# Nearer steps for the third group's tail in layer 0 of a four-layer graph attention kernel

## The chip, the cores and the metric

One core of a Trainium2 chip runs the whole kernel. Its engines are TensorE (PE), VectorE (DVE), ScalarE (ACT) and GpSimd (POOL); SP issues transfers and computes nothing. The metric is the device time of one execution in microseconds (us).

## The reference

There are 3327 nodes with 256 features and a sparse, symmetric adjacency matrix with a full diagonal. Four layers of attention follow one another; each adds its result to its input and norms the sum row by row:

```python
x = _layernorm(x + _L0_gnn_ref(x, adj, ...))   # scores from leaky_relu(g_src[i] + g_tgt[j]) @ a_w
x = _layernorm(x + _L1_gnn_ref(x, adj, ...))   # leaky_relu(s1[i] + s2[j])
x = _layernorm(x + _L2_gnn_ref(x, adj, ...))   # s_src[i] + s_dst[j]
x = _layernorm(x + _L3_gnn_ref(x, adj, ...))   # two layers of four heads each
```

In layer 0 the score of a pair of nodes needs a leaky ReLU over all 256 channels, so it can't be split into a term for each node, and it is formed only for the neighbours that exist:

```python
g = leaky_relu(g_src[:, None, :] + g_tgt[None, :, :], 0.2)
score = where(adj != 0, einsum('ijc,c->ij', g, a_w), -inf)
return softmax(score, axis=1) @ g_tgt
```

## The kernel before, in words

The nodes make 26 tiles of 128 rows. Layer 0 (`sparse0`, L288) treats them in four groups of 4, 7, 9 and 6 tiles (`SETS`); the third group is tiles 11 to 19. For each group `neighbours` lists every node's neighbours, and the nodes of a group are sorted by their number of neighbours, so that tile t of a group needs only as many places as `LEVELS` says. A tile's places are cut into parts of up to four (`parts`, L318, 237 of them). A **step** is one index q of the loop at L1370: it emits what is due at q, then the gathers of part q + 8 (`LEAD`), then the scores of part q.

What a tile passes through:

- `gather` (L916): one indirect GpSimd transfer for each place fetches one neighbour's row for 128 nodes from a table in memory. Its buffers are 22 in a ring.
- `score` (L956): VectorE takes the maximum with the own row (L946) and multiplies and sums (L952), place by place.
- `weights` (L980): VectorE finds the maximum (L985), ScalarE the exponential (L990), after the tile's last part.
- `combine` (L1013): ScalarE scales the gathered rows by their weights (L1028), PE adds them up in PSUM by a multiplication with the identity (L1031). For the very last tile, VectorE adds the parts from the fifth on instead (`add_aside`, L1007 and L1009).
- `add_input` (L1046): VectorE divides and adds the input. Its result lies in one of two buffers (tag "hs"), which `dots_next` (L1142) also uses for the weights of layer 1.
- `put_back` (L1062): an indirect GpSimd transfer writes the sums to memory in the nodes' own order. It is put into a list, `between`, from which one is taken after every second gather (L932), so it stands among the gathers of GpSimd's queue.

What a group passes through once its last tile is put back: `take` (L1073) loads the sums again from ScalarE's queue; `finish_sums` (L1081) forms mean and variance on VectorE; `finish_root` (L1103) takes the root on GpSimd; `finish` (L1109) norms on VectorE (L1114).

Then each tile is prepared for layer 1, while layer 0 goes on with later groups: `turn_next` (L1147) transposes it on PE and copies it on ScalarE, `project_next` (L1156) multiplies it by layer 1's weight on PE (L462), forms exponentials and scaled features on ScalarE (L1161 to L1166), stores them from SP's queue (L1168), and at the end of a block of tiles its rates too (L1178). The last group is normed and projected within layer 1 (`last_group`, L1398).

For the tiles of the first two groups (11 of them, `KNOWN`) layer 1's sums over each other are formed early, in the last group's time, in 44 turns from the last group's first step on: `ask_early` (L1188, SP loads), `weigh_early` (L1206, VectorE mask at L1221, ScalarE cast at L1217), `add_early` (L1226, PE at L1234) and, after each three tiles, `keep_early` (L1239), which copies three sums on ScalarE (L1242) and stores them (L1243) through two buffers.

The order is written out by hand: `at_step(q, what)` puts a call into step q, and steps beyond the last part are emitted at the end (L1386). Every engine runs its instructions in the order that they were emitted in. Within layer 0, step q's calls come in the order of their registration: combines, put-backs and finishes before transposes and projections, and these before the early turns.

The distances that the change touches are counted from a tile's last part, q: combine over steps q + 1 to q + 8 (`SPREAD`), `add_input` at q + 10, `put_back` at q + 13; for a group `take` at q + 21, `finish_sums` at q + 27, `finish_root` at q + 33, `finish` at q + 37. For the third group that last q is 181; the last group begins at step 182 and ends at step 236. The third group's transposes start at step 182 + 38 = 220 and go on every second step, each projection two steps after its transpose: 220 to 238.

Layer 1 (`one_head`, L1821) starts with the block of the first four tiles of the third group, with all 26 tiles as sources. Its first loads (a rate row, three adjacency tiles, three feature tiles; L1716, L146, L2187) come in SP's queue behind all of layer 0's loads; its pools lie in memory that layer 0 used. VectorE forms masked weights (L1728), ScalarE casts the adjacency and stores it (L1755, L146), PE adds up (L1845).

Of the kernel before, what the change touches and what calls it, by code (L numbers as in the profile page):

```python
# [32 lines left out]
SETS = (4, 7, 9, 6)  # L33
# [17 lines left out]
def gat_stack(  # L51
# [71 lines left out]
    for lo, hi in ((0, KNOWN), (KNOWN, EARLY), (EARLY, nt)):  # L123
        count = -(-(hi - lo) // 6)
# [163 lines left out]
    def sparse0(lost):  # L288
        GROUP, TURNS, LEAD, SPREAD = 4, 22, 8, 8
        starts = [sum(SETS[:s]) for s in range(len(SETS))]  # L290
        with ExitStack() as s0:
# [19 lines left out]
            def cuts_of(kt):  # L311

                ends = list(range(0, kt, GROUP)) + [kt]
                if kt % GROUP == 1:
                    ends[-2] -= 1
                return list(zip(ends, ends[1:]))
# [449 lines left out]
            between = []  # L766
# [295 lines left out]
            def put_back(s, t):  # L1062

                entry = held.pop((s, t))
                nc.gpsimd.indirect_dma_start(
                    out=sums_d[s][:, :],
                    out_offset=bass.IndirectOffsetOnAxis(
                        ap=entry["lst"][:, KMAX : KMAX + 1], axis=0
                    ),
                    in_=entry["y"][:, :], in_offset=None,  # L1070
                )
# [205 lines left out]
            ends, begins = {}, {}  # L1277
# [9 lines left out]
            def at_step(q, what, *args):  # L1287
                due.setdefault(q, []).append(lambda: what(*args))
# [17 lines left out]
            for q, key in ends.items():  # L1306
                count = len(cuts_of(seats[key]))
                if key[1] == 0:
                    at_step(q + 2, send_weights, key[0])
                    at_step(q + 3, take_weights, key[0])  # L1310
                    at_step(q + 4, combine_excess, key[0])
                for i in range(count):
                    at_step(q + 1 + i * SPREAD // max(count, SPREAD), combine, *key, i)
                at_step(q + 10, add_input, *key)
                at_step(q + 13, between.append, lambda key=key: put_back(*key))
                if key[1] == SETS[key[0]] - 1 and key[0] < len(SETS) - 1:
                    at_step(q + 21, take, key[0])
                    at_step(q + 27, finish_sums, key[0])
                    at_step(q + 33, finish_root, key[0])
                    at_step(q + 37, finish, key[0])  # L1320
            for s, q in begins.items():
                work, at = excess(s), max(q - 2, 0)
                for y in range(12):
                    at_step(at + y, go_on, work)
            at = begins[len(SETS) - 1] - 2 * KNOWN - 3
# [3 lines left out]
            for s in range(len(SETS) - 1):  # L1329
                for it in range(starts[s], starts[s] + SETS[s]):  # L1330
                    at_step(at, turn_next, it)
                    at_step(at + 2, project_next, it)
                    at += 2
                if s == len(SETS) - 3:
                    at = max(at, begins[len(SETS) - 1] + 38)
            at = begins[len(SETS) - 1] + 2
            at_step(at - 2, ask_early, 0)
            at_step(at - 1, ask_early, 1)
# [19 lines left out]
            for s in range(1, len(SETS)):  # L1358
                at = begins[s] - LEAD - 2
# [865 lines left out]
    lost = nodes.tile([P, 2 * nt], F32, name="lost")  # L2225
    nc.vector.memset(lost, 0.0)
    rest = sparse0(lost)
    with ExitStack() as rs:
        layers(rs, EARLY, rest)
# [75 lines left out]
```

## Time and profile before

| what | value |
|---|---|
| median of 3 runs | 3314.23 us (3307.76 to 3329.03) |
| profiled execution | 2906.56 us, span 2904.8 us, mean PE clock 0.887 |
| busy over the span | PE 80%, DVE 73%, ACT 30%, POOL 34% |
| last gather of layer 0 issued | 1322.4 us after the span's start |
| last put-back of layer 0 issued | 1351.7 us |
| rest (layers 1 to 3) | to 2904.8 us |

Times within the execution are us from the span's start. The page gives each engine's busy time, the span in 40 slices of 72.6 us with a digit for the busy tenths, and groups of instructions with count, busy time, mean ns of one, and the idle time before them with what ended most of it. A timeline row is start, length, engine, line, operation, output<-input, form, count, and in brackets the idle time before it and what ended it. The profiled execution is one; the runs of the median were timed without a profile.

### The profile page before, as it was taken

The page shows a single profiled execution, that of the slowest core. Times are in us where ns is not written, and L with a number is a line of the kernel's source. Part 1 is how long each engine was busy: PE and PEld are TensorE (multiplying, and loading weights), DVE is VectorE, ACT ScalarE, POOL GpSimd, SP SyncE. Part 2 cuts the span into 40 slices and gives each one's busy share as a digit, 9 for nine tenths or more (in the row PEclk, how much of TensorE's full clock was granted, in tenths as well). Part 3 has the DMA queues.
Part 4 walks back from the last instruction along what each step waited for, and adds up shares of the span by engine and source line. Part 5 has one row for each costly group of instructions (what it writes and reads, how often), then busy time and mean ns, then how long its engine had stood idle before and what let it go on. Part 6 is the DMA issues. An engine that isn't in the chain of part 4 may idle for free.

```text
span 2904.8 us, 47707 instructions
## 1 busy us (share of the span) xinstructions
PE 2310.4 (80%) x16735; PEld 1545.7 (53%) x16764; DVE 2128.0 (73%) x5634; ACT 866.0 (30%) x2441; POOL 991.7 (34%) x1059
## 2 busy tenths in 40 slices
PE   6466657555552665767899999999999999999997
PEld 4234435433442444645778888863656667534332
DVE  7799799968872856655455421158999999899997
ACT  4145445443432533544344311111011110110111
POOL 2676777777777777772000000000000000000000
PEclk9577778777776887889999999999999999999998
DMA  7795665445544557765767533331222222212211
GB/s 245 204 271 146 184 190 156 140 141 148 161 115 109 126 162 196 199 177 159 219 179 202 169 93 111 105 90 45 78 80 62 75 80 64 71 43 63 60 45 49
DMA packets 207558, 378.52 MB, mean 130 GB/s; under 512 B 38410, under 2 KB 148080, under 8 KB 206288
## 3 DMA queue, kind: packets, MB, share of 16 engines
q1 hardware_dynamic: 119416, 186.29, 22.5%
q0 software_dynamic: 50768, 154.31, 19.3%
q10 hardware_dynamic: 37128, 34.79, 3.6%
q8 instruction: 137, 2.24, 0.3%
q14 instruction: 109, 0.89, 0.1%
HBM read 333.91 MB, written 47.67 MB: 131 GB/s over the span
## 4 chain that ended last, share of the span: by engine, by line
PE 53%; DVE 8%; POOL 6%; DMA 6%; issue 5%; ACT 2%; ACTq 0%; SPq 0%; DVEq 0%; POOLq 0%; another core or an unknown queue 0%
PE acc L1913 18%; PE acc L1845 14%; PE acc L1921 9%; PE acc L1031 7%; POOL g L926 5%; DVE e L1728 3%; DMA g<-table_d,lst 3%; PE misc L1653 3%; DMA at_d<-at 1%; DVE y L952 1%; ACT g L1028 1%; DMA at<-at_d 1%; DVE y L946 1%; PE early L1234 1%; PE misc L1765 0%
## 5 line engine op out<-in xcount | busy, mean ns | idle before, releaser
L926 POOL DMA_INDIRECT g<-table_d,lst x894 | 853.9, 955 | 275.8 <-issue 237.6
L1728 DVE SCALAR_TENSOR_TENSOR e<-rate,feat,at 128x896 f32<-128x896 f32 (+4 forms) x832 | 843.4, 1078 | 59.0 <-PE acc L1921 47.8
L1913 PE MATMUL acc<-e,feat 128*32 128x384 f32 (+2 forms) x6656 | 691.5, 514 | 2.8 <-DVE e L1728 1.4
L1031 PE MATMUL acc<-g,ident 128*128 128x256 f32 x1766 | 484.5, 430 | 70.7 <-ACT g L1028 47.1
L1913 PEld LDWEIGHTS acc<-e,feat 128*32 128x32 f32 x6656 | 307.1, 110 | 294.9 <-issue 157.4
L1031 PEld LDWEIGHTS acc<-g,ident 128*128 128x128 f32 x1766 | 378.9, 219 | 158.2 <-ACT g L1028 64.9
L1921 PE MATMUL acc<-e,feat 128*32 128x384 f32 (+3 forms) x3328 | 383.6, 512 | 0.0
L1028 ACT ACTIVATE g<-g,w 128x256 f32<-128x256 f32 x883 | 367.5, 495 | 15.1 <-ACT at L1217 10.6
L946 DVE TENSOR_TENSOR y<-g,minus_ps 128x1028 f32<-128x1028 f32 (+2 forms) x233 | 273.3, 1173 | 110.0 <-DMA g<-table_d,lst 100.4
L952 DVE SCALAR_TENSOR_TENSOR y<-y,a_ps 128x257 f32<-128x257 f32 x894 | 324.6, 418 | 15.7 <-PE a_ps L810 2.2
L1845 PE MATMUL acc<-feat,e 128*128 128x257 f32 (+1 forms) x1110 | 257.5, 388 | 15.8 <-DVE e L1728 14.6
L1845 PE MATMUL acc<-feat,at 128*128 128x257 bf16 (+2 forms) x2028 | 239.3, 275 | 8.2 <-DMA at<-at_d 7.6
L1845 PEld LDWEIGHTS acc<-feat,e 128*128 128x128 f32 (+1 forms) x1110 | 211.6, 194 | 50.9 <-DVE e L1728 15.3
L1921 PEld LDWEIGHTS acc<-e,feat 128*32 128x32 f32 (+1 forms) x3328 | 162.1, 110 | 131.0 <-issue 88.7
L1845 PEld LDWEIGHTS <-at 128*128 128x128 bf16 (+2 forms) x2028 | 199.6, 100 | 42.4 <-issue 4.7
L563 PE MATMUL v<-code,leads 65*128 65x512 bf16 (+1 forms) x182 | 79.7, 438 | 144.2 <-DVE cand L589 103.3
L589 DVE MAX8 cand<-v 128x8 f32<-128x104 f32 (+2 forms) x858 | 157.1, 258 | 1.1 <-PE v L566 1.1
L1728 DVE SCALAR_TENSOR_TENSOR e<-rate,feat,at_i 128x640 f32<-128x640 f32 (+4 forms) x108 | 95.9, 899 | 82.3 <-DMA at_i<-in_adj_t_dram 27.7
L1706 POOL DMA_DIRECT2D rate3b_d<-rate_rows x4 | 2.1, 520 | 450.2 <-ACT rate_rows L1705 450.2
L1031 PE MATMUL acc<-own_of,ident 128*128 128x256 f32 x52 | 28.6, 650 | 140.3 <-ACT own_of L1028 89.8
L2099 POOL TENSOR_TENSOR rstds<-rstds,minus_half 128x7 f32<-128x7 f32 (+1 forms) x4 | 7.6, 1906 | 381.9 <-DVE rstds L2098 381.9
L261 POOL TENSOR_TENSOR rstds<-rstds,minus_half 128x6 f32<-128x6 f32 (+3 forms) x9 | 12.4, 1381 | 357.8 <-DVE rstds L260 357.8
(259 smaller groups left out, 2055.7 us busy)
## 6 DMA issues: line engine op xcount, KB each, us to landing
adj_i<-in_adj_dram SPq DMA_DIRECT2D x75, 512.0 KB
at<-at_d SPq DMA_DIRECT2D x150, 224.0 KB
at<-at_d SPq DMA_DIRECT2D x75, 192.0 KB
at<-at_d SPq DMA_DIRECT2D x75, 191.8 KB
g<-table_d,lst POOLq DMA_INDIRECT x894, 3.1
at_i<-in_adj_t_dram SPq DMA_DIRECT2D x39, 320.0 KB
at_i<-in_adj_t_dram SPq DMA_DIRECT2D x25, 383.5 KB
at_i<-in_adj_t_dram SPq DMA_DIRECT2D x25, 256.0 KB
```

The lines of the kernel that those rows point to most:

```text
L563: nc.tensor.matmul(v[:, :w], leads[:, b, :], code[:, :w], start=True, stop=False)
L589: nc.vector.max(spread[:, c0 + c, :], view(v[:, :w]))
L926: nc.gpsimd.indirect_dma_start(out=g[:, k - k0, :], out_offset=None, in_=table_d[:, :], in_offset=bass.IndirectOffsetOnAxis(ap=entry["lst" ...
L946: nc.vector.tensor_tensor(y, rows, minus_src[:, None, :].to_broadcast([P, m, dim + 1]), op=ALU.max)
L952: nc.vector.scalar_tensor_tensor(y, y, 1.0, a_ps[:, : dim + 1], op0=ALU.mult, op1=ALU.mult, accum_out=sc)
L1028: nc.scalar.activation(rows, rows, AF.Copy, scale=w[:, k : k + 1])
L1031: nc.tensor.matmul(dst, ident, rows, start=start, stop=stop)
L1653: nc.tensor.matmul(pacc[:pn, : dim + self.extra], ht[:, k, :pn], self.weight[:, k, :], start=(k == 0), stop=(k == kc - 1),)
L1728: nc.vector.scalar_tensor_tensor(e[:pn, : c1 - c0], self.rate[b][:pn, h_of, : c1 - c0], q, at[:pn, : c1 - c0], op0=ALU.max, op1=ALU.mult,)
L1845: nc.tensor.matmul(accs[s][:pn, : dim + 1], a[:pj, s * P : s * P + pn], f[:pj, : dim + 1], start=(j == skip and part == 0), stop=(j == nt ...
L1913: nc.tensor.matmul(accs[x][p][q : q + 32, : hi - lo], f[:pj, at0 : at0 + 32], es[at0 // hd][:pj, lo:hi], start=(j == 0), stop=(j == nt - 1),)
L1921: nc.tensor.matmul(accs[x][pairs][h_of * 32 : (h_of + 1) * 32, : hi - lo], f[:pj, dim + h_of : dim + h_of + 1].to_broadcast([pj, 32]), es[ ...
```

## The change

For the third group alone (`near`), the combines go over six steps instead of eight, `add_input` comes at q + 7 and `put_back` at q + 8, `take`, `finish_sums`, `finish_root` and `finish` at q + 18, 21, 23 and 26. The transposes start at step 182 + 27 = 209 and go on every step, so that they are at 209 to 217 and the projections at 211 to 219. The first two groups and the last keep their distances. No instruction is added or taken away.

```diff
+                near = key[0] == len(SETS) - 2
+                spread = 6 if near else SPREAD
                 for i in range(count):
-                    at_step(q + 1 + i * SPREAD // max(count, SPREAD), combine, *key, i)
-                at_step(q + 10, add_input, *key)
-                at_step(q + 13, between.append, lambda key=key: put_back(*key))
+                    at_step(q + 1 + i * spread // max(count, spread), combine, *key, i)
+                at_step(q + (7 if near else 10), add_input, *key)
+                at_step(q + (8 if near else 13), between.append, lambda key=key: put_back(*key))
                 if key[1] == SETS[key[0]] - 1 and key[0] < len(SETS) - 1:
-                    at_step(q + 21, take, key[0])
-                    at_step(q + 27, finish_sums, key[0])
-                    at_step(q + 33, finish_root, key[0])
-                    at_step(q + 37, finish, key[0])
+                    after = (18, 21, 23, 26) if near else (21, 27, 33, 37)
+                    for y, what in zip(after, (take, finish_sums, finish_root, finish)):
+                        at_step(q + y, what, key[0])
...
                 for it in range(starts[s], starts[s] + SETS[s]):
                     at_step(at, turn_next, it)
                     at_step(at + 2, project_next, it)
-                    at += 2
+                    at += 2 if s < len(SETS) - 2 else 1
                 if s == len(SETS) - 3:
-                    at = max(at, begins[len(SETS) - 1] + 38)
+                    at = max(at, begins[len(SETS) - 1] + 27)
```

## The prediction

> **What bounds the kernel now.** I read the page first, then busy time by stretches, then the timelines of GpSimd, ScalarE, VectorE and the SP queue around the end of layer 0. "Step" is the loop index of the schedule written out at L1370; a step scores one part of up to four neighbours.
>
> ```profile
> POOL 2676777777777777772000000000000000000000
> L926 POOL DMA_INDIRECT g<-table_d,lst x894 | 853.9, 955 | 275.8 <-issue 237.6
> ```
>
> Layer 0 fills the first 18 slices of 72.6 us. GpSimd issues 894 gathers, 0.955 us each and 0.30 us apart. 76% busy is thus its ceiling (1.0 of 1.26 us), and the stretches show it there to the end:
>
> ```profile
> 1180.00:1250.00 70.00, 39.63 (x165) 31.98 (x163) 42.20 (x141) 28.26 (x70) 53.65 (x56) 0.80 0.68 186
> 1250.00:1325.00 75.00, 54.35 (x214) 41.71 (x215) 52.20 (x172) 36.15 (x106) 56.95 (x59) 0.89 0.68 179
> 1325.00:1352.00 27.00, 22.00 (x94) 17.54 (x94) 13.42 (x41) 15.76 (x49) 1.27 (x2) 0.95 0.34 99
> ```
>
> Columns: stretch, length, busy us of PE, weight loads, DVE, ACT, POOL, then PE clock, DMA share, GB/s. POOL is at 77% and 76%, then at nothing, while PE is 81% busy: from 1325 to 1352 a tail runs that GpSimd no longer sets. GpSimd's timeline gives its ends:
>
> ```profile
> 1322.37 0.95 POOL L926 DMA_INDIRECT g<-table_d,lst  x1 [0.30 <-issue]
> 1344.59 1.00 POOL L1065 DMA_INDIRECT sums_d<-hs,lst  x1 [19.96 <-DVE aside L1007]
> 1351.73 0.96 POOL L1065 DMA_INDIRECT sums_d<-hs,lst  x1 [6.14 <-DVE counts L1392]
> ```
>
> The last gather leaves at 1322.4, the last put-back at 1351.7. Layer 1 loads its fourth feature tile at 1354.5, once that landed. The tail in VectorE, ScalarE and SP:
>
> ```profile
> 1327.62 0.96 DVE L946 TENSOR_TENSOR y<-g,minus_ps 128x771 f32<-128x771 f32 x1 [0.97 <-DMA g<-table_d,lst]
> 1329.76 0.18 DVE L985 TENSOR_REDUCE top<-sc 128x1 f32<-128x28 f32 x1
> 1335.68 1.41 DVE L1728 SCALAR_TENSOR_TENSOR e<-rate,feat,at_i 128x512 f32<-128x512 f32 x2 [5.66 <-DMA feats_d<-feat]
> ```
>
> ```profile
> 1322.79 0.37 ACT L1242 COPY part<-early 128x257 f32<-128x257 f32 x1 [3.45 <-DMA part_d<-part]
> 1330.59 0.17 ACT L1161 ACTIVATE feat<-early 128x1 f32<-128x1 f32 x1 [3.72 <-PE early L462]
> 1337.44 0.33 ACT L990 ACTIVATE w<-sc,top 128x28 f32<-128x28 f32 x1
> 1345.17 3.30 ACT L1028 ACTIVATE g<-g,w 128x256 f32<-128x256 f32 x8
> ```
>
> ```profile
> 1328.55 0.32 SPq L1716 DMA_DIRECT2D rate<-rate_d  x1
> ```
>
> The last tile's maximum is there at 1329.94, but its exponential (L990) starts at 1337.44: ScalarE still has to scale rows of the tile before, and between them waits for PE's projections of the third group (L462). Those five projections of steps 230 to 238 are what makes ScalarE and PE late.
>
> **What the Trainium skill says.** "DMA: Bandwidth & Descriptors", section "Anatomy of one DMA": a semaphore wait happens on the issuing sequencer, and most of about 2 us fixed cost is the write's receipt. The trace agrees: GpSimd itself stood 19.96 us before a put-back, and put-backs land in 2.6 to 5.9 us. "Perfetto Trace Analysis", section "Identifying the Most-Contended Engine", takes occupancy for the bottleneck. By that VectorE (70%) would be close to GpSimd (76%); here the 0.30 us between issues makes 76% a full engine, so the trace decides. "TensorE: Matmul & The Clock Gate", section "What's actually happening": PE's clock is throttled unless it is busy. The clock is 0.75 to 0.89 from 1000 to 1325 us and mostly 0.98 to 1.0 after 1500.
>
> **The change, part by part.** It adds no work. It moves instructions of the third group (nine tiles, steps 102 to 181).
>
> (a) Combining over six steps instead of eight, add_input at +7 instead of +10. Same scales (0.41 us a row) and matmuls (0.44 us a row), off GpSimd's path: 0 us. The cover is GpSimd's continuous gathers from 590 to 1323 us. If it were gone, a tile could cost two steps' rows at once, 1.7 us, times nine = 15 us.
>
> (b) put_back at +8 instead of +13. In GpSimd's queue it now stands among the gathers of step e+16, e being the tile's last part, and needs VectorE's step e+7. Everything behind it, all gathers, would wait. By counting gathers against scores in the timelines, GpSimd is 1 to 10 parts ahead; the limit falls from 11 to 9. The 10 is at step 153, where VectorE stands 40.1 us at L1142, because its buffer waits for a put-back. That put-back now comes at about 912 us instead of 939.7, so this standstill shrinks too, and VectorE resumes at about 915 instead of 942. Cost on GpSimd 0; gain 0, for it is hidden under gathers.
>
> (c) take, finish_sums, finish_root, finish at +18, 21, 23, 26 instead of +21, 27, 33, 37. take issues nine loads on ScalarE's queue (5.1 us), three steps earlier: same price, between steps of slack. finish_root is one 1.4 to 1.8 us power on GpSimd, no more than before. But VectorE's finish at step 207 must wait for it, and GpSimd reaches it just before the gathers of part 212, which began at 1196.9. VectorE would be there at 1176, so it stands until about 1198.7: 22 us, against 12.9 us at step 218 before. Then nine norms of 0.39 us, ready at 1202. Behind it wait scores only; GpSimd's gathers go on. 0 us now, a debt of four steps.
>
> (d) Transposes and projections at steps 209 to 219, one tile a step, instead of 220 to 238. Each brings its SP store of features and, twice, of rates, placed ahead of that step's early loads on SP. From the chain around 1271: projection 0.89, four activations 0.72, transposes 0.45, copy 0.37, early cast and store 0.80, four scales 1.7, last row 0.45: 5.4 us a step, against GpSimd's 5.1. So eleven steps end at about 1199.5 + 11 × 5.4 = 1259. With keep_early's wait (5 us) at step 220, step 222's rows end near 1273 (1271.2 before). From there no projection is left: 3.4 us a step instead of 4.4, so step 230's first row comes near 1299 instead of 1304.3.
>
> (e) The tail. keep_early of step 232 starts near 1306 instead of 1318.2, its third copy goes out near 1311, and the rows of steps 233 to 236 (16 × 0.41 = 6.6 us) are scaled before the last gather lands at 1327.6. The last gather itself doesn't move. So the exponential follows the maximum: 1330.7 (with one hoisted op, below) instead of 1337.4, **6.7 us**. From it to the last row it took 12.0 us (1349.4) with a projection in between; now 0.5 + 19 rows × 0.41 + 0.47 = 8.8, **3.2 us**. VectorE's side sum (5.5 us) fits beside it. Sum 9.9 us.
>
> (f) The instruction order of VectorE also changes: the first two layer-1 mask ops (L1728), after the last scores before, now stand inside the scores of parts 235 and 236. They need layer-1 loads that SP issues only when keep_early's last store has landed (5.0 us after its issue), and come 7.1 us after that (1328.55 to 1335.68). With SP free at 1316 they are ready at 1323, ahead of their turn at 1325: cost 0.7 us, counted.
>
> After the tail, layer 1's loads, stores and matmuls keep their order and shift as a whole. Against the profiled execution: 2906.6 − 9.9 = 2896.7. The runs shown have a median 408 us (14%) longer; no view says where those lie. If all stretched alike the gain would be 11.3. I take 10: **3304 us**, 0.3% less.
>
> **The rivals.**
>
> *It stays hidden or is half eaten* (0 to 5 us, about 3311). For it: VectorE starts the nine steps with a 22 us debt, and (d) estimates eleven dependent steps to within 5 us. Against it: 17 steps without projections follow.
>
> *The hoisted mask ops hold the last scores.* If SP gets free at R, the maximum comes at R + 7.1 + 5.1 (two mask ops 1.4, two scores' rest 3.7). Up to R = 1318.5 nothing is lost. At R = 1328.5, where SP got free before, the gain is all gone; beyond it each microsecond is lost time. Ten later gives 3324. For it: a lower clock than the profiled one lengthens (d) most. Against it: five projections less between step 222 and 232.
>
> *More than the tail is won.* If in the runs shown VectorE or PE, not GpSimd, holds parts of layer 0, then (b)'s 27 us (942 to 915) become real: 3314 − 10 − 27 = 3277. Against it: not one gather of the profiled execution from 590 us on waited more than 0.45 us.
>
> *GpSimd stalls at a nearer put-back*: unlikely. The nearest is that of step 159, which GpSimd reaches at about 960; VectorE, resuming at 915 with 2.65 us a step, has its sums by about 936.
>
> **How the numbers follow.** Forecast (6 to 14 us off, 3300 to 3308) 0.55; half eaten 0.2; hoisted ops, slower than before, 0.13 (3315 to 3330); more won 0.12 (3275 to 3298). The range leaves out the far ends of the last two: 3287 to 3324; the likeliest's own is 3300 to 3308. About 1% (33 us) is what a measurement of this kernel can tell from no change. Faster by that 0.07, from the last case's end; slower 0.03, from the mask ops more than 40 us late; same 0.90.
>
> **What would show it.** Right: gathers still end near 1322, no layer-0 projection after 1262, exponential within 1 us of the maximum, last put-back near 1342, same length from there to the end. Wrong: L926 or L1065 waiting for VectorE before 1320; L1728 standing between L946 and L952; the copy at L1242 after 1315; a changed distance from the last put-back to the end.

## The result, and the profile after

The changed kernel takes 3374.44 us (median of 4 runs, 3364.26 to 3376.65) beside 3318.66 us of the kernel before (4 runs, 3307.76 to 3329.03): ratio **1.0153** [1.0111, 1.0196]; brackets behind a ratio hold its 95% interval. The forecast was 3304 in a range of 3287 to 3324. The time went up instead of down, and lies outside the range.

One plain fact is needed to read what follows. The kernel before took about 2907 us in two of the six series of experiments, with a spread of under 20 us over 58 runs, and 3310 to 3331 us (medians) in the others; one chip gave one level in one series and the other in a later one. The profile that the prediction was worked out from (2906.56 us) is of the first kind. The runs that the median was shown for, and the profile of the changed kernel (3376.65 us, span 3374.8), are of the second. I call them the *even* and the *broken* condition. All ratios compare runs within one series.

The page of the changed kernel, GpSimd's line of busy tenths and its gathers:

```profile
POOL 2734645656555555535650000000000000000000
L926 POOL DMA_INDIRECT g<-table_d,lst x894 | 853.7, 955 | 398.3 <-issue 263.2
```

The gathers take what they took (853.7 us against 853.9), but GpSimd stands 398.3 us before them instead of 275.8, and its row of sevens is gone. So the prediction's "not one gather … waited more than 0.45 us" does not hold here. The kernel before, profiled in the broken condition (the run b_before), has 435.7 us there. It, and not the page shown ahead of the prediction, is the kernel to compare with. Busy time by stretches, of b_before and then of the changed kernel: from the gather of part 101, the last one before the third group, to the last gather; to the last put-back; to the end (columns as in the prediction):

```profile
821.00:1714.00 893.00, 429.62 (x1453) 319.63 (x1461) 460.40 (x1713) 272.10 (x734) 531.54 (x556) 0.69 0.44 119
1714.00:1788.00 74.00, 58.68 (x251) 45.98 (x250) 48.58 (x153) 41.19 (x125) 3.36 (x4) 0.95 0.32 90
1788.00:3336.00 1548.00, 1492.12 (x13710) 952.76 (x13709) 1104.72 (x1518) 290.08 (x898) 33.02 (x35) 0.99 0.34 97
```

```profile
814.00:1761.00 947.00, 432.84 (x1530) 320.76 (x1530) 464.02 (x1723) 282.17 (x777) 532.18 (x556) 0.70 0.42 113
1761.00:1825.00 64.00, 45.96 (x183) 37.11 (x182) 47.79 (x153) 32.29 (x81) 3.47 (x4) 0.88 0.30 88
1825.00:3374.00 1549.00, 1494.68 (x13715) 954.72 (x13713) 1105.25 (x1518) 290.41 (x898) 33.46 (x36) 0.99 0.34 97
```

The busy time of GpSimd is equal (531.54 and 532.18 us). The first stretch grows by 54 us, the tail shrinks by 10 us. Layers 1 to 3 stay: from the last put-back to the end it is 1549.8 and 1550.7 us, and 1553.1 us in the even profile. The two spans differ by 38.2 us. The changed kernel reaches part 101 some 7 us earlier, by chance, as it is the same program up to there; the loss is made in the third and the last group of layer 0, and a gain at the tail of about the forecast's size is there beside it. What GpSimd waited for in the first stretch, of b_before and then of the changed kernel (us in total, times, longest):

```profile
POOL sums_d L1065 <- DVE hs L1056: 51.5, 10, 8.7
POOL g L926 <- remote: 46.6, 15, 5.0
POOL sums_d L1065 <- DVE seat L807: 22.8, 2, 11.4
```

```profile
POOL sums_d L1065 <- DVE hs L1056: 146.2, 13, 25.2
POOL g L926 <- remote: 36.1, 12, 5.8
POOL sums_d L1065 <- DVE seat L807: 15.4, 1, 15.4
POOL rstd L1105 <- DVE rstd L1100: 13.7, 1, 13.7
```

GpSimd stands at put-backs (L1065) for VectorE: 161.6 us instead of 74.3, most of it put down to the sums (L1056), up to 25.2 us at one. "PSUM — Partial Sum Buffer", section "Engine vs sequencer instructions", of the Trainium skill says that GpSimd's queue is strictly first in, first out. The trace agrees: below, the gather at 1398.25 starts only behind the put-back at 1396.93, which had stood 19.3 us. One of these waits in the timeline of the changed kernel, engine after engine (rows of ScalarE, PE, VectorE and GpSimd):

```profile
1378.63 0.17 ACT L1161 ACTIVATE feat<-early 128x1 f32<-128x1 f32 x1 [40.13 <-remote]
1382.44 4.89 ACT L1028 ACTIVATE g<-g,w 128x256 f32<-128x256 f32 x12
1383.00 7.25 PE L1031 MATMUL acc<-g,ident 128*128 128x256 f32 x24 [42.26 <-ACT g L1028]
1395.71 0.48 DVE L1052 SCALAR_TENSOR_TENSOR hs<-acc,inv,own_of 128x256 f32<-128x256 f32 x1 [23.95 <-PE acc L1031]
1396.93 1.01 POOL L1065 DMA_INDIRECT sums_d<-hs,lst  x1 [19.32 <-DVE hs L1056]
1398.25 0.96 POOL L926 DMA_INDIRECT g<-table_d,lst  x1 [0.30 <-issue]
```

ScalarE stands 40 us at a projection's exponential, and the profile names nothing that ended the wait ("remote"). Its scales come late, so PE stands 42 us for them, VectorE 24 us for PE's sums, GpSimd 19 us for VectorE, and the next gather comes only then. What a put-back far behind the sums would have kept from GpSimd, the near one hands on. The largest waits without a named releaser, over all engines of the changed kernel from 100 to 1800 us:

```profile
DVE y L952 <- remote: 163.5, 31, 10.1
PE v L563 <- remote: 117.3, 9, 28.0
ACT feat L1161 <- remote: 110.5, 5, 40.1
```

The kernel before in the broken condition has them too (33 kinds of them in that window); the profile ahead of the prediction has a single one, of 0.3 us.

What two of these waits are for can be read all the same. The exponential at 1378.63 reads a bank (`early`) that PE's L462 had written. VectorE's L952 reads what the instruction just before it on VectorE itself, L946, had written. Rows of PE and VectorE of the changed kernel:

```profile
1339.49 1.03 PE L462 MATMUL early<-w,ht 128*128 128x258 f32 x4
1340.36 0.38 PE L1150 MATMUL early<-ident,h 128*128 128x128 f32 x2
1359.70 1.23 DVE L946 TENSOR_TENSOR y<-g,minus_ps 128x1028 f32<-128x1028 f32 x1 [1.31 <-issue]
1368.83 0.42 DVE L952 SCALAR_TENSOR_TENSOR y<-y,a_ps 128x257 f32<-128x257 f32 x1 [7.90 <-remote]
```

The same pair of VectorE in the profile ahead of the prediction:

```profile
999.76 1.22 DVE L946 TENSOR_TENSOR y<-g,minus_ps 128x1028 f32<-128x1028 f32 x1
1001.01 0.42 DVE L952 SCALAR_TENSOR_TENSOR y<-y,a_ps 128x257 f32<-128x257 f32 x1
```

In the broken condition PE's matmuls were over at 1340.74 (a modelled end) and L946 at 1360.93. The trace has the semaphore updates that released the next ones, a semaphore being the counter by which one instruction tells another that it is done, at 1378.61 and 1368.80: 38 and 8 us later. So, as recorded, it is the signal that came late here, even from an engine to itself. Between L946 and L952 VectorE stands 249 us in all in the changed kernel, and 22 us in the profile ahead of the prediction.

### The profile page after: what moved, and what is told of

Read it like the earlier page. It is cut to its first block, busy times and chain, and to the rows that moved or that the text cites. A ratio compares the mean times of both kernels' runs of the same rounds, so it can differ in the third digit from the quotient of the medians.

```text
span 3374.8 us, 47748 instructions
## 1 busy us (share of the span) xinstructions
PE 2376.9 (70%) x16764; PEld 1577.1 (47%) x16764; DVE 2141.2 (63%) x5634; ACT 868.3 (26%) x2441; POOL 992.8 (29%) x1059
## 4 chain that ended last, share of the span: by engine, by line
PE 46%; DVE 16%; another core or an unknown queue 12%; issue 11%; POOL 6%; DMA 5%; ACT 3%; SPq 0%; ACTq 0%; DVEq 0%; POOLq 0%
PE acc L1914 16%; PE acc L1846 12%; PE acc L1922 8%; POOL g L926 5%; PE acc L1031 5%; DVE y L952 4%; DVE y L946 3%; DVE e L1729 2%; PE misc L1654 2%; ACT g L1028 2%; DVE cand L589 2%; DMA g<-table_d,lst 1%; DVE found L597 1%; DVE junk L688 1%
## 5 line engine op out<-in xcount | busy, mean ns | idle before, releaser
L926 POOL DMA_INDIRECT g<-table_d,lst x894 | 853.7, 955 | 398.3 <-issue 263.2
L1031 PE MATMUL acc<-g,ident 128*128 128x256 f32 x1766 | 531.6, 459 | 253.0 <-ACT g L1028 168.3
L1031 PEld LDWEIGHTS acc<-g,ident 128*128 128x128 f32 x1766 | 407.1, 236 | 366.4 <-ACT g L1028 187.1
L952 DVE SCALAR_TENSOR_TENSOR y<-y,a_ps 128x257 f32<-128x257 f32 x894 | 324.7, 419 | 224.5 <-remote 163.5
L946 DVE TENSOR_TENSOR y<-g,minus_ps 128x1028 f32<-128x1028 f32 (+2 forms) x233 | 273.2, 1172 | 28.4 <-issue 23.0
L589 DVE MAX8 cand<-v 128x8 f32<-128x104 f32 (+2 forms) x858 | 168.4, 261 | 86.0 <-issue 78.5
L563 PEld LDWEIGHTS <-leads 65*128 65x128 bf16 x182 | 22.1, 121 | 266.2 <-remote 108.3
L261 POOL TENSOR_TENSOR rstds<-rstds,minus_half 128x6 f32<-128x6 f32 (+3 forms) x9 | 12.4, 1383 | 361.3 <-DVE rstds L260 361.3
```

The lines of the kernel that those rows point to most:

```text
L563: nc.tensor.matmul(v[:, :w], leads[:, b, :], code[:, :w], start=True, stop=False)
L589: nc.vector.max(spread[:, c0 + c, :], view(v[:, :w]))
L926: nc.gpsimd.indirect_dma_start(out=g[:, k - k0, :], out_offset=None, in_=table_d[:, :], in_offset=bass.IndirectOffsetOnAxis(ap=entry["lst" ...
L946: nc.vector.tensor_tensor(y, rows, minus_src[:, None, :].to_broadcast([P, m, dim + 1]), op=ALU.max)
L952: nc.vector.scalar_tensor_tensor(y, y, 1.0, a_ps[:, : dim + 1], op0=ALU.mult, op1=ALU.mult, accum_out=sc)
L1031: nc.tensor.matmul(dst, ident, rows, start=start, stop=stop)
```

## The experiments

"Lead" is by how many parts GpSimd may be ahead of VectorE before a put-back holds it: a put_back emitted at e + x stands among the gathers of part e + x + 8 and needs VectorE's add_input of step e + y, so x + 8 − y: before 11, after 9. The theories: **L**, what costs is the lead that is left when engines stand at unforeseen places; **C**, the crowded norms and projections cost; **N**, any change of the order shifts such waits. All edits below are against the kernel before unless said otherwise; the third group is meant by "near".

The first series splits the change. b_before is the kernel before, unaltered. e_front has only the first half of the change (spread 6, add_input +7, put_back +8), norms and projections as before. Against the changed kernel:

```diff
-                    after = (18, 21, 23, 26) if near else (21, 27, 33, 37)
+                    after = (21, 27, 33, 37)
...
-                    at += 2 if s < len(SETS) - 2 else 1
+                    at += 2
...
-                    at = max(at, begins[len(SETS) - 1] + 27)
+                    at = max(at, begins[len(SETS) - 1] + 38)
```

> The kernel before, unchanged, for a second profile. Its profiled execution (2906.6 us) lies 12% under its timed runs (3308 to 3329), while the changed kernel's profiled execution (3376.7) lies at its own. Theory L (lead): in the timed runs VectorE, ScalarE and PE stand for hundreds of us in layer 0 with no releaser that the profile shows, GpSimd runs to the end of its lead and waits at put-backs. Then this profile, if it is an execution of about 3315 us, ends layer 0's gathers near 1700 instead of 1322, and GpSimd waits at the third group's put-backs, but clearly less than the 144 us of the changed kernel. Rival C (crowding): GpSimd waits there as long as in the changed kernel, and the difference lies in steps 207 to 222. Ratio 1.00.

> Only the first half of the change: for the third group combine over six steps, add_input at +7, put_back at +8; take, sums, root, norms and projections where they were before. Theory L: this half holds the loss, ratio 1.010 to 1.018. Rival C (crowding of norms and projections): ratio 0.995 to 1.004. Rival N (any new order of instructions shifts the waits that have no releaser): both halves off 1 by an amount unlike their sum, sign open.

e_back has only the second half (norms at +18, 21, 23, 26, projections from +27, one apart); e_put13 is the whole change but for the put-back. The latter against the changed kernel:

```diff
-    at_step(q + (8 if near else 13), between.append, lambda key=key: put_back(*key))
+    at_step(q + 13, between.append, lambda key=key: put_back(*key))
```

> Only the second half: put-backs as before (+10, +13, combine over eight steps), but take at +18, sums at +21, root at +23, norms at +26, and the nine projections one step apart from step 209. Theory L: ratio 0.995 to 1.005, since only the root (one wait on GpSimd) comes nearer. Rival C: ratio 1.010 to 1.018, with the time lost between steps 207 and 222. Rival N: as for the other half.

> The changed kernel with the third group's put_back alone back at +13 (add_input stays at +7). GpSimd then meets each put-back five parts later, six steps after its sums are due. Theory L: the nine waits of 4 to 25 us at these put-backs go, and with them most of the loss: ratio 0.997 to 1.006. Rival C: ratio stays at 1.010 to 1.018. Rival N: anything between 0.99 and 1.02.

Measured: b_before 0.9994 [0.9978, 1.001]; e_front 1.0148 [1.0105, 1.0192]; e_back 1.004 [1.0026, 1.0053]; e_put13 1.0044 [1.0026, 1.0062]. The first half alone loses as much as the whole change, and moving the one put-back away again takes 1.1% of 1.5% off. C is worth 0.4%.

The second series asks whether it is the lead or the place of the put-back, and what the 0.4% is. b_put11 shortens the lead without any other move; e_put10 puts the changed kernel's put-back where the lead is as before; e_rootv is e_back with the root taken from GpSimd; b_all713 gives more lead to all groups by early sums:

```diff
-    at_step(q + 13, between.append, ...)      # b_put11: 11 for the third group
-    at_step(q + (8 if near else 13), ...)     # e_put10, in the changed kernel: 10
+    nc.scalar.activation(rstd, rstd, AF.Sqrt) # e_rootv, in finish_root
+    nc.vector.reciprocal(rstd, rstd)
-    at_step(q + 10, add_input, *key)          # b_all713: 7 and spread 6 for every group
```

> Before with one change: the third group's put_back at +11 instead of +13, add_input still at +10. It stands among the gathers of step e + 19 and needs VectorE's step e + 10, so GpSimd may lead by 9 parts, as in after (before: 11), but the put-back itself is only two of after's five steps earlier. L (what counts is the lead that is left): about the whole of the put-back's cost in after, 1.008 to 1.012. Rival W (the earlier write itself costs, by its place): two fifths of 1.1%, 1.004.

> After with the third group's put_back at +10 instead of +8, add_input still at +7. It stands among the gathers of step e + 18 and needs VectorE's step e + 7: a lead of 11 parts, as in before, though it is three steps earlier than before. L: the put-back's cost is gone, what is left is the second half's 0.4%: 1.003 to 1.006. W: three fifths of 1.1% and 0.4%: 1.011.

> The second half of the change alone (as e_back, which measured 1.004), with the third group's root taken out of GpSimd's queue: ScalarE takes the square root, VectorE the reciprocal. If the 0.4% is GpSimd standing at the root (13 to 18 us at L1105 in after and e_back, nothing in before): 0.999 to 1.001, and no L1105 wait. If it is the crowded norms and projections on VectorE, ScalarE and PE: 1.004 as e_back. ScalarE may need some us to change its function and back, which no run has shown yet; that would count on the second side.

> Before with the sums of every group combined over six steps and add_input at +7, while put_back stays at +13 for all: the lead that put-backs allow grows from 11 to 14 parts, and gathered rows come free earlier. L: fewer waits at L1065 in all groups, some move to L926, a gain: 0.990 to 0.999. If the leads of before are long enough already: 1.000. Rival N (any change of order costs): 1.002 to 1.005.

Measured: b_put11 1.0127 [1.0066, 1.0187], a little over what L said; W's 1.004 (the place of the put-back costs, not the lead) lies outside the interval. e_put10 1.0086 [1.0062, 1.011], between both, with W's 1.011 at the interval's edge: L is too simple there. e_rootv 1.0036 [1.002, 1.0052] without a wait at L1105. Its price is two loads of ScalarE's tables of 1.28 us each (ACT_TABLE_LOAD), too little for the 0.4% (about 12 us), so the root is not what most of the second half costs. b_all713 1.0151 [1.0098, 1.0204]: L said a gain, and was wrong. Its put-backs hardly wait any more (17.0 us), but VectorE stands 194.8 us at add_input (L1052), against 88.5 in b_before; more than half of it has no named releaser (111.4 us).

The third series takes b_all713 apart and turns the change round: e_add7 has early sums in the third group alone, b_all6 only the denser combines, b_all16 only a later put-back for every group:

```diff
-    at_step(q + 13, between.append, lambda key=key: put_back(*key))
+    at_step(q + 16, between.append, lambda key=key: put_back(*key))
```

> Before with the third group's combines over six steps and its add_input at +7 alone; put_back stays at +13, norms and projections as before. Theory A (an early add_input stands on VectorE for PE's sums, one step after the last combine instead of two): VectorE stands at L1052 in the third group for more than 100 us (before: 47, the kernel with put_back alone back at +13: 128) and the ratio is 1.003 to 1.006. Theory L alone (only put_backs cost, and here they have 14 parts of lead instead of 11): 0.998 to 1.001.

> Before with the combines of every group over six steps, add_input and put_back untouched. The kernel that also had add_input at +7 everywhere measured 1.0151. A (the early add_input is what costs there): 0.998 to 1.003, VectorE stands at L1052 no longer than in before. Rival S (the denser combines cost, on ScalarE and PE): about 1.015.

> Before with put_back of every group at +16 instead of +13: the allowed lead grows from 11 to 14 parts, nothing else moves. L: GpSimd's waits at L1065 for VectorE (35 us in the third group, 17 in the last) nearly vanish, part of them moves to gathers that wait for PE to free a buffer; 0.992 to 0.999. Rival: the ring of 22 buffers limits the lead to about 12 parts anyway: 0.999 to 1.001.

Measured: e_add7 1.0014 [1.0000, 1.0028]; b_all6 1.0166 [1.0147, 1.0185]; **b_all16 0.994 [0.9919, 0.9961]**, faster than both kernels. VectorE's waits at add_input in e_add7, from 822 to 1748 us:

```profile
DVE hs L1052 <- remote: 62.6, 5, 30.9
DVE hs L1052 <- PE acc L1031: 49.6, 3, 27.3
DVE hs L1052 <- issue: 23.0, 1, 23.0
```

Theory A's wait is there (142.4 us with a 7.2 us one, against 88.5 in b_before), but it costs 0.1%, less than A said. Rival S is right for b_all6: six steps for the combines of *all* groups cost 1.7%, and its put-backs wait 134.4 us though its lead is 11, as before. Why this is dear in the other groups and free in the third I can't say. N, as it was put for b_all713 (any new order costs), does not fit b_all16, which is a new order too and gains. And GpSimd in b_all16, as above, third and last group:

```profile
POOL g L926 <- PE acc L1031: 68.2, 16, 12.9
POOL g L926 <- remote: 65.3, 21, 6.7
POOL g L926 <- DVE found L597: 13.4, 1, 13.4
POOL sums_d L1065 <- DVE seat L807: 3.9, 2, 3.6
```

The line L1065 <- L1056 is gone. A part of it has become gathers that wait for PE to free a buffer of the ring. The measures together, for all fourteen profiled executions in the broken condition ("standing" is GpSimd's at L1065 for other engines, from part 101 to the last gather; length is that stretch; a_after and b_all16b are the changed kernel and b_all16 once more, told of below):

| kernel | lead of the third group | standing, us | length, us | tail, us | ratio |
|---|---|---|---|---|---|
| changed | 9 | 161.6 | 948 | 63.5 | 1.0153 |
| a_after | 9 | 157.0 | 950 | 63.9 | 1.0187 |
| e_front | 9 | 155.1 | 934 | 73.4 | 1.0148 |
| b_all6 | 11 | 134.4 | 929 | 74.6 | 1.0166 |
| b_put11 | 9 | 126.8 | 911 | 73.7 | 1.0127 |
| e_put10 | 11 | 109.8 | 917 | 62.2 | 1.0086 |
| e_back | 11 | 78.1 | 902 | 63.4 | 1.004 |
| b_before | 11 | 74.3 | 893 | 73.3 | 0.9994 |
| e_rootv | 11 | 65.1 | 898 | 62.6 | 1.0036 |
| e_put13 | 14 | 50.8 | 901 | 63.6 | 1.0044 |
| e_add7 | 14 | 37.2 | 886 | 76.4 | 1.0014 |
| b_all713 | 14 | 17.0 | 887 | 76.6 | 1.0151 |
| b_all16b | 14 | 6.5 | 870 | 71.8 | 0.9977 |
| b_all16 | 14 | 4.8 | 873 | 71.8 | 0.994 |

The standing and the length fall together, 157 us of the one for 75 of the other; with less standing a part of the time is spent waiting elsewhere. b_all713 fits in length and not in ratio, so its loss lies outside this stretch; where, its profile doesn't show in full. Its combines are denser in the first two groups too, and its gather of part 101 comes at 827 us, that of b_all6 at 843 us, against 806 to 822 us in the ten profiles whose first two groups are unaltered. The profiled execution of a kernel lies up to 0.4% beside its median (e_back's is 12 us under it), so the 0.4% of the second half can't be placed by them.

The fourth series was to place it, and to find the end of the gain: e_norm has the second half's norms without its projections, b_put16 the third group's put-back alone at +16, b_all18 all at +18.

> Before with the third group's take, sums, root and finish alone at +18, +21, +23 and +26; its transposes and projections stay at steps 220 to 238, two apart, its put_back at +13. If the second half's 0.4% comes from the norms (VectorE's waits for the loads and the root, GpSimd at the root): 1.003 to 1.005. If it comes from the projections coming nearer and one a step: 0.999 to 1.001.

> Before with the third group's put_back alone at +16 instead of +13 (lead 14 instead of 11). L: the third group's 35 us at L1065 nearly vanish, part comes back as gathers that wait for a buffer; every group at +16 measured 0.994, so one group of four: 0.996 to 0.999. If only put-backs nearer than +13 matter in this group: 1.000.

> Before with put_back of every group at +18 (allowed lead 16; take at +21 still comes after it). At +16 GpSimd already stood less than 4 us for sums in the third and last groups, and stood for PE to free a buffer instead. L with the ring as the next limit: as at +16, 0.992 to 0.996. If leads still matter: under 0.992. If a later put-back delays the take: over 0.996.

Here the kernel before took 2907.7 us: the even condition. Measured: e_norm 0.9985 [0.9977, 0.9993], b_put16 1.0005 [0.9996, 1.0014], b_all18 1.0002 [0.9992, 1.0011]. Where no engine stands for unseen reasons, more lead is worth nothing, as the prediction's dismissal of put-back waits said for its own profile. What the second half costs in the broken condition stays open; e_norm was not measured there.

Last, the changed kernel twice more, once beside b_all16 again:

> The changed kernel itself, unaltered. Where before takes about 2907 us and its gathers don't stand: the prediction's own working, 9.9 us less, 0.995 to 0.999. Where before takes 3315 to 3330: 1.011 to 1.020 as first measured.

> Before with put_back of every group at +16 once more, on the same chip as the changed kernel. Where before takes about 2907 us: 0.999 to 1.001, as at +18. Where before takes 3315 to 3330: 0.991 to 0.997 as first measured.

> The changed kernel itself, unaltered, once more. Where before takes about 2907 us: the prediction's own working, 9.9 us less, 0.995 to 0.999, and no wait of GpSimd at L1065 between 600 and 1320 us. Where before takes 3315 to 3330: 1.011 to 1.022.

The first two fell into the broken condition (before 3310.36 us): a_after 1.0187 [1.0155, 1.022], b_all16b 0.9977 [0.996, 0.9994], a smaller gain than was expected of it. The third fell into the even one (before 2907.68 us): a_after2 2911.28 us, **1.0012 [1.0001, 1.0023]**. So the gain of 9.9 us does not come even there, and the loss of 1.5% is the broken condition's alone.

## Why the prediction was wrong

**The base.** "Not one gather of the profiled execution from 590 us on waited more than 0.45 us" was true, and in a_after2 GpSimd's put-backs stand 0.9 us in all between part 101 and the last gather. The failed step is the sentence "no view says where those [408 us] lie … I take 10". The prediction worked out a gain in one execution and put it on a median 14% higher, as though the missing 408 us could not touch the change. Its rival "More than the tail is won" did ask what happens if VectorE or PE hold parts of layer 0 there, but found only a gain in it, not a put-back that waits for them. b_before shows where the time lies: layer 0 ends at 1786.8 us instead of 1351.7, all of the difference, in waits that pass from engine to engine (the busy times of VectorE, ScalarE and GpSimd agree within 10 us in the two profiles).

**(b) put_back, and its rival.** "Cost on GpSimd 0" and "GpSimd stalls at a nearer put-back: unlikely" decided the sign. The margin, "limit falls from 11 to 9", was named rightly, with a seen lead of up to 10. In the broken condition that margin is what counts: 161.6 us of standing against 74.3. Both directions were measured: the near put-back alone costs (b_put11, 1.3%), and taking it away from the change mends most of it (e_put13). Its other part was right in the even condition: VectorE's stand at L1142 ended at 918.3 us in a_after2, forecast 915, and gained nothing.

**(a) add_input and combines** cost 0 to 0.3% in the third group (e_add7), although VectorE stands longer at add_input.

**(c)** VectorE's stand at the norms was forecast as 22 us and measured 20.9 us in a_after2; GpSimd's gathers went on meanwhile. GpSimd's own wait at the root (13.7 us in the changed kernel) is not what most of the second half costs (e_rootv).

**(d)** The last projection of layer 0 starts at 1264.2 us in a_after2; the forecast had the eleven steps ended near 1259 and none after 1262. Right to 5 us.

**(e) and (f), the tail.** In a_after2, whose lines below 1312 are one further, GpSimd, VectorE, ScalarE and SP's queue:

```profile
1326.14 0.96 POOL L926 DMA_INDIRECT g<-table_d,lst  x1 [0.30 <-issue]
1346.95 0.99 POOL L1065 DMA_INDIRECT sums_d<-hs,lst  x1 [18.55 <-DVE aside L1007]
1354.09 0.97 POOL L1065 DMA_INDIRECT sums_d<-hs,lst  x1 [6.16 <-DVE counts L1393]
1333.14 0.75 DVE L1729 SCALAR_TENSOR_TENSOR e<-rate,feat,at_i 128x512 f32<-128x512 f32 x1 [6.02 <-DMA at_i<-in_adj_t_dram]
1337.85 0.18 DVE L985 TENSOR_REDUCE top<-sc 128x1 f32<-128x28 f32 x1
1345.72 0.48 DVE L1052 SCALAR_TENSOR_TENSOR hs<-acc,inv,own_of 128x256 f32<-128x256 f32 x1 [7.62 <-PE acc L1031]
1307.70 0.32 ACT L990 ACTIVATE w<-sc,top 128x31 f32<-128x31 f32 x1 [3.21 <-DVE top L985]
1316.13 0.38 ACT L1242 COPY part<-early 128x257 f32<-128x257 f32 x1 [1.77 <-PE early L1234]
1338.07 0.32 ACT L990 ACTIVATE w<-sc,top 128x28 f32<-128x28 f32 x1 [11.66 <-DVE top L985]
1323.62 0.32 SPq L1717 DMA_DIRECT2D rate<-rate_d  x1
```

The exponential follows the maximum, as forecast. But the maximum itself is late: a mask op of layer 1 stands 6 us between the last scores for its load, since SP comes free at 1323.6 where 1316 was forecast. SP is late because keep_early is: its first copy (L1242) starts at 1316.1 where 1306 was forecast, only 2 us earlier than before. "3.4 us a step" without projections was too short a step: ScalarE, freed of them, waits for VectorE's maximum of the tile before (3.2 us at 1307.7) and for PE. From the last gather to the exponential it is 11.9 us, before 15.1: 3.1 gained instead of 6.7. That is the rival of the hoisted mask ops, on a small scale. From the exponential to the last put-back it is 16.0 us, before 14.3: 1.7 lost instead of 3.2 gained. ScalarE's rows were done 8.0 us behind the exponential, even sooner than the 8.8 of the forecast, but "VectorE's side sum … fits beside it" was wrong: it stands behind the add_input of the tile before (L1052), which waits 7.6 us for PE. Together 1.4 us instead of 9.9; the last gather comes 3.8 us later than in the profile of before, and 5 and 6 us later in two of the three other kernels of that condition, so that part need not be the change's.

In the broken condition the tail is shorter by the sum that was forecast, 63.5 us against 73.3; it is 62 to 64 us in all six executions with the second half, 72 to 77 us in all eight without. The exponential of b_before and of the changed kernel:

```profile
1772.46 0.33 ACT L990 ACTIVATE w<-sc,top 128x28 f32<-128x28 f32 x1
1807.17 0.32 ACT L990 ACTIVATE w<-sc,top 128x28 f32<-128x28 f32 x1 [7.35 <-DVE top L985]
```

The way was the forecast's: with the projections gone, the exponential waits for the maximum alone. The match in size is luck. Up to the exponential it is 46.6 us instead of 59.0, 12.4 gained and not 6.7; behind it 16.9 instead of 14.3, 2.6 lost where 3.2 gained were forecast. The 54 us ahead of the tail swallow it.

One reading of the prediction was a little off, without weight: the put-backs whose landing its profile shows take 2.45 to 5.93 us, not 2.6 to 5.9.

What stays open is why the signals come late. Waits without a named releaser are absent from the five profiles in the even condition, but for the one of 0.3 us, and one of the five is of a chip that showed the broken condition earlier. The transfers themselves are not slower: the packets of the gather queue take 174 to 177 ns in the mean in both, in the third and the last group. One rival is not excluded, the recording itself. Up to the last put-back the traces of the broken condition hold 9,205 to 9,837 semaphore updates, those of the even one 26,168 to 26,240, though the kernels have the same work; behind it all hold 14,582 to 14,591. So records are missing in just the stretch where the time is lost. The first runs of the kernel before were timed without a profile, it is said ahead of the prediction, and lay at 3308 to 3329 us, which speaks against it; but the record lists a span and a granted clock for every later timed run, so it isn't shown that runs without any recording stand as long. Whether recording holds the engines up, or something else causes the waits and the missing records alike, no run here separates.

## What to carry to other kernels

Before working out a gain, set the profiled execution's time against the median: the 12% between them meant here that the profile was of another regime, and that a margin which it shows as idle was what the timed runs live on. In an engine's queue that runs in order, an instruction that needs another engine's result should stand so far behind that result that the producer may be late; moving it nearer saves nothing where that engine never waits, and hands delays on where it does. Here moving it farther, +16 instead of +13, gained 0.2 to 0.6% in the broken condition and showed no loss in the even one (measured there at +16 for the third group and at +18 for all).

## What the runs showed of the hardware

- The same kernel on the same chip has two levels in different series, 2907 and 3315 us; runs of one level within a series lie within about 1% of each other. All of the difference lies in layer 0; from the last put-back to the end every execution takes 1549 to 1559 us.
- "Perfetto Trace Analysis", section "Optimization Strategy", of the Trainium skill says to look for the gaps on the engine of interest and for the semaphore that ends them. Here that led through four engines to a 40 us gap. The semaphore that ends it is one that PE's matmuls raise, and its update is recorded 38 us behind the end of the last of them. No instruction transfer landed in the gap: the DMA queues of the changed kernel from 1340 to 1379 us list none.
- PE's clock was granted as 0.69 and 0.70 in the first stretch of the broken condition, and 0.77 and 0.78 in the even one, where PE has the same work in less time.
- ScalarE loads a table when it changes to the square root and again when it goes back to the exponential: 1.28 us each, at 1559.99 and 1615.51 us of e_rootv.
